# Edge scores of a graph network: ScalarE's copies for two tiles put ahead of others, VectorE's passes over fetched tiles placed in the units beside the last layer's chain

## The chip, the cores and the metric

The kernel runs on one core of a Trainium2 chip. The metric is the device time of one launch in microseconds (us). The median of three runs of the kernel before is 3469.57 us (3468.32 to 3470.26).

## The reference

64 graphs of 256 nodes with 256 features each go through four layers: first layer, second layer, attention, last layer (GNN[0], GNN[1], the attention layer, and LAST in the code). All graphs share one sparse 256x256 adjacency matrix. The first, second and last layer compute the same thing with weights of their own:

```python
pre_u = jnp.einsum('bud,dk->buk', h_t, W1[:d])
pre_v = jnp.einsum('bvd,dk->bvk', h_t, W1[d:])
hidden = jax.nn.relu(pre_u[:, :, None, :] + pre_v[:, None, :, :] + b1)
S = jax.nn.sigmoid(jnp.einsum('buvk,ko->buvo', hidden, W2)[..., 0] + b2[0])
a_t = jnp.einsum('buv,bud->bvd', S * A_a, h_t)
m_t = jnp.einsum('uv,bud->bvd', A_m, h_t) * h_t
z_t = beta1 * h_t + beta2 * (a_t @ Wa + ba) + beta3 * (m_t @ Wm + bm)
```

(The last line is shortened: the two products there are einsums.) The score S is wanted only where the adjacency matrix is not zero. The attention layer forms logits from one projected value per node, takes a softmax along the masked rows and adds the weighted features to its input.

## The kernel before, in words

**Edges.** At its start the kernel counts the edges and makes selection matrices from them. The edges off the diagonal are packed into tiles of up to 128 edges. For one edge the kernel needs pu of one node plus pv of the other, then a pass relu times W2 summed along the features. There are three ways to it. For the tiles in FAST, ScalarE copies rows of pu and pv into `pre` (rows_u, rows_v), and TensorE adds the pair of each edge with a selection matrix `pick` into a PSUM tile `ga`. For the tiles in FETCHED, POOL gathers rows from tables in HBM: tableu first, then tablev added on top of it (fetch, line 824). For the diagonal, `own` is pu + pv of the same node (itself). The few remaining edges share one gathered tile, `left`. Every tile holds two graphs, so it takes two VectorE passes (rated, both; in the profile `junk<-ga`, `junk<-fetched`, `junk<-own`, `junk<-left`), each of which writes one column of `raw`.

**From scores to sums.** rated_all turns a set of columns into `val` on ScalarE (tanh, then + 1) and on VectorE into `rm`. It is called twice in a unit: for EARLY, when the first half of the columns is there, and for LATE at the end. early() puts the remaining edges and the diagonal into `sa` (matmuls `ps<-ro,guo`). spread() brings `rm` into matrix form with 32 small matmuls in two halves (`ps<-rm,gu`) and adds it to `sa`. finish() forms sa x h, the output products and z.

**Streams and units.** Two streams, a and b, take two graphs each at a time, in 16 rounds. beside(heavy, light, placed) lays the scores of one stream's layer (heavy) beside the other stream's chain (light): the rest of its layer after the scores (after), attention, and the start of its next layer (before: pu, pv, tables in HBM, first copies into `pre`). Six such units make up a round. In the order of time the heavy parts are: a's first layer, b's first, a's second, b's second, a's last, b's last. The light chain is a generator; every step yields how many FAST tiles (made) and how many fetched tiles (got) are traced at that point. STEPS (line 45) holds these numbers for finish(), the list `beside` (line 656) those for before(). Beside b's last layer and a's first layer the light chain is the other stream's last layer and the start of its next graphs' first layer.

**What sets the order.** The order in which an engine issues its instructions is not the order of the code. A scheduler picks, per engine, among the instructions that its model holds to be ready, the one traced first. `issue_after(x)` adds an order behind x on x's engine, with no semaphore. With placed=True, `stay` puts TensorE's ga tiles, VectorE's passes and the EARLY tanh behind what was traced just before them on their engine, the diagonal is done beside the first two fetched tiles, and early() comes right after the EARLY ratings; otherwise the diagonal is done beside FAST tiles 1 and 2, the EARLY ratings come when all FAST tiles are traced, and early() follows the sixth fetched tile. In the kernel before, placed is True beside b's first layer and beside a's second.

**Names that matter.** FAST tile n uses pre[:, n]. before() calls rows_u(0, 2) and rows_v(4, 2) after its first half of nodes, and rows_v(0, 2) after its second. made() calls rows_u and rows_v for tiles 2n + 2 and 2n + 3, on ScalarE behind past[-1], the last rating of the unit before. `itself` does the diagonal. POOL's list of gathers (FETCHES) is one order across all units; the first six of a unit are issued in before(), behind the table writes of SP's queue (line 677), and the others at the start of the unit.

Of the kernel before, what the change touches and what calls it, by code (L numbers as in the profile page):

```python
# [17 lines left out]
GNN = ("L0_gnn_", "L1_gnn_", "L3_gnn_")  # L18
LAST = GNN[2]
# [25 lines left out]
STEPS = {  # L45
    GNN[0]: [(1, 1), (1, 1), (0, 1), (1, 0), (0, 1), (2, 1)],
    GNN[1]: [0, 0, 0, (0, 1), (0, 1), 1],
    LAST: [1, 1, (0, 1), (1, 1), (0, 1), (2, 1)],
}

VEC = {}
# [11 lines left out]
def blk(c):  # L63
    return slice(c * P, (c + 1) * P)
# [37 lines left out]
def adj_seq_kernel(ctx: ExitStack, tc: tile.TileContext, a: dict, out: bass.AP):  # L102
# [15 lines left out]
    tensor, vector, scalar = Noting(nc.tensor), Noting(nc.vector), Noting(nc.scalar)  # L118
# [383 lines left out]
    def few(stack):  # L502
# [139 lines left out]
        def more(st, l):  # L642

            return (st["side"], l) in (("a", LAST), ("b", GNN[1]))

        def before(st, l):

            hT = st["hT"]
            pu = one.tile([P, 2, 2, D], FP, tag="pu" + st["side"], name="pu")
            pv = one.tile([P, 2, 2, D], FP, tag="pv" + st["side"], name="pv")  # L650
            pre = one.tile([P, len(FAST), 2 * D], FP, tag="pre" + st["side"], name="pre")
            order = [(m, g) for m in range(2) for g in range(2)]
            if l == LAST:
                order = [(m, g) for g in range(2) for m in range(2)]

            beside = {LAST: [0, (0, 1), (0, 1), (0, 1)], GNN[1]: [0] + [(0, 1)] * 3, GNN[0]: [0, 0, (0, 2), (0, 1)]}[l]
            beside = dict(zip(order, beside))
            st["tables"] = [
                tables.tile([N, 2 * D], FP, tag="table" + t + st["side"], name="table" + t) for t in "uv"
            ]  # L660

            st["pu"], st["pv"], st["pre"] = pu, pv, pre
            if l != GNN[1]:
                st["own"] = one.tile([P, 2, 2, D], FP, tag="own", name="own")
            t = one.tile([P, FIRST, 2, D], FP, tag="fetched" + st["side"], name="fetched")
            st["fetched"] = [t[:, f] for f in range(FIRST)]
            for m, g in order:
                if l == LAST and (m, g) == (1, 0):
                    st["flip"](1)
                t = psum()  # L670
                for c in range(2):
                    mm(out=t, lhsT=hT[:, c, g, blk(m)], rhs=w1[l][:, c], start=c == 0, stop=c == 1)
                scalar.copy(pu[:, m, g, :], t[:, 0, :])
                vector.tensor_tensor(pv[:, m, g, :], t[:, 1, :], b1row[l], ALU.add)
                if g == 1:
                    for rows, x in zip(st["tables"], (pu, pv)):
                        nc.sync.dma_start(out=rows[blk(m)], in_=flat(x)[:, m])
                    if m == 0:
                        st["fetches"] = list(FETCHES_MORE if more(st, l) else FETCHES)

                        if numbered:
                            fetch(st, AHEAD)
                if l != GNN[1]:
                    vector.tensor_tensor(st["own"][:, m, g, :], t[:, 0, :], pv[:, m, g, :], ALU.add)
                if g == 1:
                    if m == 0:
                        rows_u(st, 0, 2, 0, 0)
                    rows_v(st, 4 - 4 * m, 2, 0)
                yield beside[(m, g)]
                if l == GNN[1] and (m, g) == (0, 1):  # L690
                    st["turn"](0)
                    yield 0, 1
                    st["turn"](1)
                    yield 0
            yield REST_OF_IT

            yield from mixed(st, l, later if past else None, (0,) if more(st, l) else (0, 1))

        def scores(st, l, placed):
# [3 lines left out]


            stay = behind if placed else lambda engine: nullcontext()
            pre = st["pre"]
            raw = wk.tile([P, LATE.stop], FP, tag="raw", name="raw")
            val = wk.tile([P, LATE.stop], FP, tag="val", name="val")
# [24 lines left out]
            def tile_scores(t, k, m, i):  # L733
                col = BLOCKS + 16 * m + 4 * k + i
                both(t, col, col + 8)
# [25 lines left out]
            def made():  # L761
                for n, (k, m, i) in enumerate(fast):
                    t = ga.tile([P, 2, D], FP, tag="ga", name="ga")
                    with stay(tensor):
                        mm(out=t, lhsT=pick[:, k, 4 * m + i, :], rhs=pre[:, n], start=True, stop=True)
                    tile_scores(t, k, m, i)
                    if 2 * n + 2 < len(fast):

                        with tc.issue_after(past[-1]) if past else nullcontext():
                            rows_u(st, 2 * n + 2, 2, *FAST[2 * n + 2][:2])  # L770
                            if n != 1:
                                rows_v(st, 2 * n + 2, 2, FAST[2 * n + 2][0])
                    if n in (1, 2) and not placed:
                        itself(n - 1)
                    count.append(n)
                    yield
                    if n == 2 and more(st, l):
                        yield from mixed(st, l, None, (1,), ga)

            def got(made):  # L780
                for f, block in enumerate(blocks):
                    if f == FIRST:
                        if placed:
                            while len(count) < 4:
                                next(made)
                        else:
                            for _ in made:
                                yield
                        with stay(vector):
                            rated(left, REST)  # L790
                        rated_all(EARLY, 0)
                        yield
                        if placed:
                            early(st)
                            yield
                    if f < 2 and placed:
                        itself(f)
                    with stay(vector):
                        tile_scores(fetched[f], *block)
                    if f == FIRST + 1 and not placed:  # L800
                        early(st)
                    yield
# [4 lines left out]

            made = made()
            return made, got(made), end

        def fetch(st, n):

            now, st["fetches"] = st["fetches"][:n], st["fetches"][n:]
            for f, x in now:
                rows = st["tables"][x]
                if f < 0:
                    to, ids = st["left"], (left_u, left_v)[x]
                    rows = rows.rearrange("n (g d) -> (n g) d", g=2)
                else:
                    to, ids = st["fetched"][f].rearrange("p g d -> p (g d)"), (ids_u, ids_v)[x][:, f : f + 1]  # L820
                    if f < FIRST:
                        rows = rows[blk(0)]
                with tc.issue_after(fetches[-1]) if fetches else nullcontext():
                    this = nc.gpsimd.indirect_dma_start(  # L824
                        out=to, out_offset=None, in_=rows, in_offset=bass.IndirectOffsetOnAxis(ap=ids, axis=0),
                        compute_op=(ALU.bypass, ALU.add)[x],
                    )
                fetches.append(this.ins)
# [9 lines left out]
        def rows_v(st, f, n, k):  # L838

            for n in range(f, f + n):  # L840
                i = FAST[n][2]
                scalar.copy(
                    st["pre"][halves[1 - k], n], st["pv"][halves[i % 2], i // 2].rearrange("p g d -> p (g d)")
                )
# [37 lines left out]
        def stream(side, starts):  # L882

            sts = [{"b": b, "side": side} for b in starts]
            load(sts[0])
            short = [before(sts[0], GNN[0])]
            for i, st in enumerate(sts):
                yield short, (st, GNN[0]), False
                yield [after(st, GNN[0]), before(st, GNN[1])], (st, GNN[1]), True
                yield [after(st, GNN[1]), attention(st), before(st, GNN[2])], (st, GNN[2]), False  # L890
                short = [after(st, GNN[2])]
                if i + 1 < len(sts):
                    load(sts[i + 1])
                    short = [halfway(after(st, GNN[2]), 4, before(sts[i + 1], GNN[0]), 2)]
            yield short, None, False
# [29 lines left out]
        past, numbered, fetches, later = [], [], [], []  # L925
# [119 lines left out]
```

## Time and profile before

| | |
|---|---|
| median of three runs | 3469.57 us |
| the profiled execution | 3468.32 us |
| its span | 3466.6 us |
| PE (matmuls) busy | 3361.7 us |
| VectorE (DVE) busy | 2639.6 us |
| POOL busy | 2416.1 us |
| weight loads (PEld) busy | 2067.6 us |
| ScalarE (ACT) busy | 1557.2 us |
| one copy pre<-pu for two tiles, mean | 1044 ns |
| one copy pre<-pv for one tile, mean | 616 ns |
| one pass over a fetched tile's graph, mean | 419 ns |
| one gather from tableu / tablev on POOL, mean | 1014 / 1583 ns |

The span is the time from the first to the last instruction. A row of the waits view reads "engine, what it was about to do, what it waited for: us in total, times, longest". A row of the timeline reads "start in us from the span's start, us, engine, operation, output<-inputs, count", and in brackets the engine's idle time before it with what ended it. Matmuls are pipelined, so that a matmul's bar is longer than the distance to the next one. An FP32 matmul in the code is two in the profile.

### The profile page before, as it was taken

To read this page: it belongs to the slowest core of one execution; us is meant where nothing else is said; L and a number is where in the kernel's file an instruction comes from. 1 tells how busy PE (TensorE), PEld (TensorE's weight loads), DVE (VectorE), ACT (ScalarE), POOL (GpSimd) and SP (SyncE) were. 2 spreads that over 40 slices of the span, in tenths; PEclk is the share of its full clock that TensorE was granted. 3 is DMA by queue.
4 is the path that set the end of the run, shared out by engine and by line. 5 is a ranking of instruction groups with operands and counts; after the bars stand their busy time and mean duration, and the time that the engine had idled before them with its cause. 6 is when DMAs were issued, how large, how long until landed. Compare 5 with 4: busy or idle time off the path is not lost.

```text
span 3466.6 us, 48384 instructions
## 1 busy us (share of the span) xinstructions
PE 3361.7 (97%) x14200; PEld 2067.6 (60%) x14200; DVE 2639.6 (76%) x10523; ACT 1557.2 (45%) x2833; POOL 2416.1 (70%) x1882
## 2 busy tenths in 40 slices
PE   6999999999999999999999999999999999999998
PEld 3566565565656566565665656656565665656655
DVE  5777787777777777777777877777777777777776
ACT  2444444444444444444444444444444444444442
POOL 3767777677767767677677776777767676776765
PEclk7999999999999999999999999999999999999999
DMA  5788787877878778787787877878787787877875
GB/s 148 164 185 188 166 207 164 193 176 178 197 168 196 179 178 186 176 196 171 178 188 165 197 170 187 183 170 205 167 196 173 178 197 165 193 179 175 190 162 129
DMA packets 289070, 620.81 MB, mean 179 GB/s; under 512 B 39072, under 2 KB 56352, under 8 KB 288800
## 3 DMA queue, kind: packets, MB, share of 16 engines
q0 software_dynamic: 204800, 461.49, 65.2%
q1 hardware_dynamic: 82416, 154.96, 12.8%
q8 instruction: 115, 1.88, 0.2%
q10 hardware_dynamic: 1584, 1.20, 0.1%
q14 instruction: 155, 1.27, 0.1%
HBM read 500.06 MB, written 117.44 MB: 178 GB/s over the span
## 4 chain that ended last, share of the span: by engine, by line
PE 68%; POOL 9%; DMA 7%; issue 7%; DVE 6%; ACT 3%; ACTq 0%; POOLq 0%; DVEq 0%
PE ps L79 52%; PE ga L79 16%; POOL fetched L824 8%; DMA fetched<-tablev,ids_v 4%; DVE junk L79 3%; ACT pre L79 2%; DMA fetched<-tableu,ids_u 2%; DVE rm L79 1%; DMA tableu<-pu 1%; POOL left L824 1%; DVE sa L79 1%; ACT val L79 1%; ACT pu L79 1%; DVE own L79 0%; DVE pv L79 0%
## 5 line engine op out<-in xcount | busy, mean ns | idle before, releaser
L824 POOL DMA_INDIRECT fetched<-tablev,ids_v x832 | 1317.3, 1583 | 381.1 <-issue 257.0
L824 POOL DMA_INDIRECT fetched<-tableu,ids_u x832 | 843.7, 1014 | 547.1 <-DMA tableu<-pu 286.7
L79 DVE SCALAR_TENSOR_TENSOR junk<-fetched,L_gnn_w2row 128x256 f32<-128x256 f32 x1664 | 643.0, 419 | 171.3 <-DMA fetched<-tablev,ids_v 167.3
L79 PE MATMUL ga<-pre,pick 128*128 128x512 f32 x1408 | 723.5, 609 | 37.0 <-ACT pre L79 27.4
L79 PE MATMUL ps<-L_gnn_w,hT 128*128 128x512 f32 x1536 | 708.0, 598 | 5.7 <-DMA hT<-in_xT_dram 5.7
L79 DVE SCALAR_TENSOR_TENSOR junk<-ga,L_gnn_w2row 128x256 f32<-128x256 f32 x1408 | 538.3, 419 | 103.7 <-PE ga L79 92.2
L79 PEld LDWEIGHTS ps<-L_gnn_w,hT 128*128 128x128 f32 x1536 | 280.6, 191 | 323.7 <-issue 300.2
L79 ACT COPY pre<-pv 64x512 f32<-64x512 f32 x704 | 434.0, 616 | 72.6 <-DVE pv L79 49.3
L79 PE MATMUL ps<-sa,h 128*128 128x256 f32 x1536 | 363.7, 382 | 13.2 <-DVE sa L79 8.9
L79 PEld LDWEIGHTS ps<-sa,h 128*128 128x128 f32 x1536 | 292.5, 191 | 126.0 <-issue 68.5
L79 ACT COPY pre<-pu 64x1024 f32<-64x1024 f32 x352 | 361.6, 1044 | 8.0 <-DVE ids_v L79 0.6
L79 PEld LDWEIGHTS ga<-pre,pick 128*128 128x128 f32 x1408 | 249.2, 191 | 184.4 <-issue 91.3
L79 ACT COPY pu<-ps 128x256 f32<-128x256 f32 x384 | 142.8, 372 | 481.3 <-PE ps L79 430.8
L79 ACT ACTIVATE hb<-hT,L_gnn_zbias,scas 128x512 f32<-128x512 f32 x128 | 97.3, 807 | 477.9 <-DVE hT L79 354.5
L79 DVE TENSOR_TENSOR rm<-gva,val 128x256 f32<-128x256 f32 x768 | 280.1, 420 | 33.1 <-ACT val L79 24.2
L79 PE MATMUL ps<-adj,h 128*128 128x256 f32 x1280 | 297.2, 384 | 4.0 <-issue 4.0
L79 PEld LDWEIGHTS ps<-adj,h 128*128 128x128 f32 x1280 | 242.1, 191 | 73.7 <-issue 40.3
L79 DVE TENSOR_TENSOR pv<-ps,L_gnn_b1row 128x256 f32<-128x256 f32 x384 | 161.7, 421 | 134.5 <-ACT pu L79 125.6
L79 PEld LDWEIGHTS ps<-rm,gu 128*64 128x64 f32 x3072 | 175.1, 138 | 135.2 <-issue 50.3
L79 ACT COPY aT<-ps 128x512 f32<-128x512 f32 x192 | 112.4, 585 | 315.9 <-PE ps L79 284.6
L79 PE MATMUL ps<-rm,gu 128*64 128x128 f32 x3072 | 218.7, 281 | 23.0 <-DVE rm L79 22.6
L79 PE MATMUL ps<-aT,L_gnn_Wa 128*128 128x512 f32 x512 | 240.6, 592 | 0.0
(149 smaller groups left out, 4211.8 us busy)
## 6 DMA issues: line engine op xcount, KB each, us to landing
tableu<-pu SPq DMA_DIRECT2D x192, 256.0 KB
tablev<-pv SPq DMA_DIRECT2D x192, 256.0 KB
hT<-in_xT_dram SPq DMA_DIRECT2D x32, 512.0 KB
h<-in_x_dram SPq DMA_DIRECT2D x64, 256.0 KB
out_dram<-h SPq DMA_DIRECT2D x64, 256.0 KB
fetched<-tableu,ids_u POOLq DMA_INDIRECT x832
fetched<-tablev,ids_v POOLq DMA_INDIRECT x832
L_gnn_w<-in_L_gnn_W_dram SPq DMA_DIRECT2D x6, 256.0 KB
```

The costliest lines, as they stand in the source:

```text
L79: self.last = getattr(self.engine, op)(*a, **k)
L824: this = nc.gpsimd.indirect_dma_start(out=to, out_offset=None, in_=rows, in_offset=bass.IndirectOffsetOnAxis(ap=ids, axis=0), compute_op=( ...
```

## The change

Three edits stand in the diff. First, before() notes its last copy into `pre` as st["rows"], and made() puts the copies for tiles 2 and later behind it on ScalarE. Second, placed becomes True beside a's first layer from the second round on (`i > 0`). The same value is used beside b's last layer of every round but the last through the stream's next step: both units have the other stream's last-layer chain as their light part. What the diagonal does is split off: only b's first layer and a's second (diagonal_later) keep it beside the fetched tiles. Third, the step lists of the last layer's finish() and of the first layer's before() change where fetched tiles are traced.

```diff
-    LAST: [1, 1, (0, 1), (1, 1), (0, 1), (2, 1)],
+    LAST: [1, (1, 1), 0, (1, 1), (0, 1), (2, 1)],
...
-            beside = {LAST: [0, (0, 1), (0, 1), (0, 1)], GNN[1]: [0] + [(0, 1)] * 3, GNN[0]: [0, 0, (0, 2), (0, 1)]}[l]
+            beside = {LAST: [0, (0, 1), (0, 1), (0, 1)], GNN[1]: [0] + [(0, 1)] * 3, GNN[0]: [(0, 1)] * 4}[l]
...
                         rows_u(st, 0, 2, 0, 0)
                     rows_v(st, 4 - 4 * m, 2, 0)
+                    st["rows"] = scalar.last.ins
...
+            diagonal_later = placed and (st["side"], l) in (("b", GNN[0]), ("a", GNN[1]))
...
-                        with tc.issue_after(past[-1]) if past else nullcontext():
+                        with tc.issue_after(past[-1]) if past else nullcontext(), tc.issue_after(st["rows"]):
                             rows_u(st, 2 * n + 2, 2, *FAST[2 * n + 2][:2])
...
-                    if n in (1, 2) and not placed:
+                    if n in (1, 2) and not diagonal_later:
                         itself(n - 1)
...
-                    if f < 2 and placed:
+                    if f < 2 and diagonal_later:
                         itself(f)
...
-                yield short, (st, GNN[0]), False
+                yield short, (st, GNN[0]), i > 0
```

## The prediction

> **What bounds the kernel now.** I call a unit by its heavy stream and layer (a-first, b-first, a-second, b-second, a-last, b-last, the order in time; 16 rounds). A unit ends where ScalarE rates its last score columns (the 128x16 tanh into val); fifteen rounds between such marks give 211.4 us each.
>
> First the page's busy times, then the view of waits for TensorE's matmul row (total us, times, longest):
>
> ```profile
> PE 3361.7 (97%) x14200; PEld 2067.6 (60%) x14200; DVE 2639.6 (76%) x10523; ACT 1557.2 (45%) x2833; POOL 2416.1 (70%) x1882
> ```
>
> ```profile
> PE ga L79 <- ACT pre L79: 27.4, 25, 2.3
> PE ps L79 <- DVE rm L79: 22.6, 27, 6.0
> ```
>
> TensorE is the bound and its visible waits are small: what can be won is in these two rows. A busy row hides part of a wait, so I took starts of successive matmuls from the timeline and subtracted the usual spacing (429 ns after 128x512, 216 after 128x256, 54 after one of the rm,gu pairs). What is over 350 ns per gap sits at unit starts: a-last 16 gaps, 1.23 to 2.55 us, 27.4 us in all; b-last 16 gaps, 8.3 us (0.47 to 0.90); b-first 16 gaps, 13.8 us (mostly 0.65). The rest is scattered, or in the first 100 and last 30 us.
>
> Then the timeline at the start of one a-last unit, ScalarE and then TensorE (start, us, instruction, count, idle time before):
>
> ```profile
> 1463.20 0.22 ACT L79 ACTIVATE val<-val 128x16 f32<-128x16 f32 x1
> 1463.44 1.04 ACT L79 COPY pre<-pu 64x1024 f32<-64x1024 f32 x1
> 1464.51 2.53 ACT L79 COPY pre<-pv 64x512 f32<-64x512 f32 x4
> ```
>
> ```profile
> 1465.18 1.12 PE L79 MATMUL ga<-pre,pick 128*128 128x512 f32 x2 [1.04 <-ACT pre L79]
> 1466.23 1.09 PE L79 MATMUL ps<-rm,gu 128*64 128x128 f32 x16
> 1467.26 1.13 PE L79 MATMUL ga<-pre,pick 128*128 128x512 f32 x2
> ```
>
> The first edge tile (ga) starts when the first pre<-pv copy ends (1465.13). In front of that copy stands pre<-pu, the 1.04 us copy for tiles 2 and 3, which nobody needs yet. The order is the same at all 16 starts of a-last and b-last; at the other four kinds of start both pv copies are already done before the tanh.
>
> Last, TensorE at the start of one b-first, and of the a-first of the same round:
>
> ```profile
> 1570.43 1.09 PE L79 MATMUL ps<-rm,gu 128*64 128x128 f32 x16
> 1571.96 1.42 PE L79 MATMUL ps<-rm,gu 128*64 128x128 f32 x16 [0.43 <-issue]
> ```
>
> ```profile
> 1539.37 1.13 PE L79 MATMUL ga<-pre,pick 128*128 128x512 f32 x2
> 1540.93 1.42 PE L79 MATMUL ps<-rm,gu 128*64 128x128 f32 x16 [0.44 <-DVE rm L79]
> ```
>
> The second half of the spread waits for rm, which follows val, which follows VectorE's last passes over fetched tiles. a-first (free order) fills with a ga tile; b-first (placed) can't.
>
> **What the skill says.** The Trainium skill, "TensorE: Matmul & The Clock Gate", Architectural detail, calls ScalarE's and VectorE's queues strict FIFO: the trace agrees (pv stood 1.04 us behind pu though ready). "Perfetto Trace Analysis", Identifying the Most-Contended Engine, says that matmul busy time is no good measure of headroom and weight-load time is; here 60% against 97%, but most of the distance is spacing that no reordering removes. "DMA: Bandwidth & Descriptors", Anatomy of one DMA — SWDGE path, gives 2.0 us + bytes/436 GB/s, an estimate of 2.6 us for 256 KB. From the trace's DMA records (each gather ends with sixteen 4-byte packets) a v gather here takes 4.7 us from issue to the last of them (4.2 to 6.0), a u gather 3.8: the measured ones are used. The same page, Two DMAs through the same engine are not ordered, asks for a wait between dependent transfers: POOL's 127.8 us of waits on u gathers agree.
>
> **The change, part by part.** Waits other than those named stay as they are.
> 1. ScalarE's edge (copies for tiles 2 on behind the copies for tiles 0 and 1). It adds no instruction. At a-last the order becomes v0, v1, u2, v2, v3. v0 ends at 1463.44 + 0.62 = 1464.06, so the first ga runs from 1464.11, not 1465.18. The spread's second half follows at 1465.16, but rm's third pass ends at about 1465.2: 1465.26 against 1466.23. Next ga tile: v1 done at 1464.70, no wait. Gain 0.95 a start, x16 = 15.2 us. In starts with a 2.5 us gap VectorE was late with pv behind a fetch; the 1.04 us comes off all the same. At b-last, v0 would end at 1505.27 and TensorE is busy until 1505.91: the whole 0.47 to 0.50 goes, x16 = 7.5 to 8. u2 and v2 are needed at 1508.5 and end by 1507.6. What is queued behind the edge is u2 alone, whose tiles come later.
> 2. Placed order in b-last and in a-first from round two. At the start of a-first the ga tile no longer fills the gap: it is pinned behind the spread. From b-first, placed today, I read: with rm in time, sums of A times h (sa,h) start 2.80 us after the spread's first half; with rm late, 1.74 + 3.17 = 4.91 us after val. Today's free a-first needs some 4.4 us for the same work undelayed, so fewer switches win about 0.4 to 0.7.
>    VectorE's tail after the last pv of a-first holds half a tile's passes, own, four sa (1.65), two tiles (1.4): 4.0 us to val. Placed: own and three tiles, 0.34 + 3 x 0.69 = 2.4, since the early ratings and sa move to mid-unit, into idle times of 2.17 and 1.27 us. So val comes up to 1.3 us sooner, but not before the last gather's landing + 1.2 us (the least seen). Now val follows that landing by 1.2 to 4.2 us at b-last (under 1.8 in 7 of 15 rounds) and 1.3 to 4.7 at a-first.
>    Taking the later of the two for each round, with TensorE 0.5 us earlier from part 1: a-first's start loses 4.7 us over 15 rounds (in the example landing 1537.4, val 1538.6, sa,h 1543.5 against 1543.25), b-first's start gains 11.9 (sa,h 1574.2 against 1575.13), a-second's loses 0.7.
> 3. The step lists (last layer: f0 beside the second aT, and so on; first layer: one fetched tile per step) only place VectorE passes and cost no instruction. The mid-unit tiles land ahead of their slot by 0.6 us or more (b-last in one round: f1 to f3 landed 12.9, 15.6, 18.3 us after the start; their slots, behind the two pv and the first output's matmuls, are at about 14.5, 16.3, 19). If a landing is later, pv or the output sum waits; TensorE has three ga and five ps buffers in front.
>    Round one's a-first stays free; its end follows the last landing by 1.8 us: 0, at worst +-2.
>    No DMA is added or moved past another: POOL's list is the same, and gathers start from table writes that come earlier with TensorE.
>
> Sum: 15.2 + 7.5 (fifteen b-lasts; the sixteenth is swallowed by the tail's landings) - 4.7 + 11.9 - 0.7 = 29 us. With VectorE's advance only 0.6 us, the same working gives 21. I take 25: the profiled execution goes from 3468.3 (span 3466.6, 1.7 around it) to 3443.3; the median of the runs stands 1.3 above it, so 3444.5.
>
> **The rivals.**
> - Only ScalarE's edge pays, 0.27: the gathers of b-last, a-first and b-first run back to back on POOL from one table write, so val cannot come sooner, and pinned ga tiles lose what b-first wins. For: seven b-last rounds have val at 1.2 to 1.8 after landing. Against: b-first's gap of 0.65 is there also where the lag is 3 us. Time 3450 to 3463, about 3455.
> - Strict placing turns landings into VectorE stalls, slower, 0.12: a gather that lands after its slot blocks pv and the table write behind it, so the next unit's gathers start later, and the delay returns. Today's placed units show the wait (junk on fetched, 167.3 us, 129 times) without TensorE stopping. It decides above 23/30 = 0.77 us of TensorE idle in each of the 30 newly placed units (23 being part 1's gain); at 1.5 us it is 30 x 1.5 - 23 = +22, 3491.
> - The edge does nothing, because the issue order that comes out has pu first or another stall in the place (rm at a-last is only 0.1 us behind), and placing nets zero: 0.06, 3463 to 3476.
>
> **How the numbers follow.** Likeliest case 0.55 (3430 to 3450; own range); the others 0.27, 0.12, 0.06. A measurement tells from no change about 0.2%, 6.9 us. Faster: 0.55 + 0.27 = 0.82; same 0.06; slower 0.12. The range 3430 to 3466 leaves out the slower case, half of the unchanged one and a small tail below.
>
> **What would show it.** Right: pre<-pv twice directly after val at a-last and b-last; PE ga on ACT pre from 27.4 to under 10 us; a-last's starts 0.9 shorter; the rm wait at b-first gone; four sa and the early val some 5 us earlier in b-last and a-first. Wrong: a new rm gap of about 1 us at a-first's start; junk-on-fetched waits growing by over 60 us with pv behind them; b-first's gap unchanged.

## The result and the profile after

The changed kernel takes 3462.8 us (median; 3458.0 to 3467.5) beside 3468.3 us for the kernel before on the same chip: ratio 0.9985, 95% interval 0.9976 to 0.9994. That is 5.5 us less, within the 0.2% that a measurement tells from no change, where 25 us less were predicted. Measured again in the first set below, the ratio is 0.9980 (0.9969 to 0.9991), so a small gain is real.

The profiled execution took 3460.8 us (span 3459.1). Its busy times:

```profile
PE 3354.6 (97%) x14200; PEld 2069.3 (60%) x14200; DVE 2649.2 (77%) x10523; ACT 1555.9 (45%) x2833; POOL 2414.1 (70%) x1882
```

The largest waits of TensorE's matmul row, and VectorE's wait for fetched tiles (total us, times, longest):

```profile
PE ps L79 <- DVE rm L79: 18.6, 10, 5.8
PE ps L79 <- DVE sa L79: 18.2, 16, 2.3
PE ga L79 <- ACT pre L79: 16.0, 16, 1.7
...
DVE junk L79 <- DMA fetched<-tablev,ids_v: 179.5, 134, 3.8
```

The wait of ga on pre fell from 27.4 to 16.0 us, not to under 10. The wait on rm hardly fell (22.6 before), and the one on sa doubled (8.9 before).

The timeline at the start of one a-last, ScalarE and then TensorE; it is the same round as the one shown of the kernel before:

```profile
1465.72 0.22 ACT L79 ACTIVATE val<-val 128x16 f32<-128x16 f32 x1
1465.96 1.26 ACT L79 COPY pre<-pv 64x512 f32<-64x512 f32 x2
1467.12 1.04 ACT L79 COPY pre<-pu 64x1024 f32<-64x1024 f32 x1
...
1465.59 0.65 PE L79 MATMUL ps<-rm,gu 128*64 128x128 f32 x6
1466.63 1.13 PE L79 MATMUL ga<-pre,pick 128*128 128x512 f32 x2 [0.39 <-ACT pre L79]
1467.69 1.74 PE L79 MATMUL ps<-rm,gu 128*64 128x128 f32 x26
```

ScalarE's order is the one predicted: two pv copies directly behind val. TensorE's order is not. Before, the ga tile stood behind 16 matmuls of the spread; now it stands behind 6, with 26 after it. The scheduler picks the tile earlier (I take it that its model now holds the tile ready earlier; this was not looked at), so less work covers the wait that is left.

TensorE at the starts of one a-first and one b-first:

```profile
1325.03 1.02 PE L79 MATMUL ga<-pre,pick 128*128 128x512 f32 x2
1325.98 1.09 PE L79 MATMUL ps<-rm,gu 128*64 128x128 f32 x16
1328.98 1.22 PE L79 MATMUL ps<-rm,gu 128*64 128x128 f32 x15 [1.90 <-DVE rm L79]
...
1572.81 2.35 PE L79 MATMUL ps<-rm,gu 128*64 128x128 f32 x32
```

b-first's spread now runs through without a wait (32 in a row). At a-first the wait for rm stands in the middle of the spread, up to 3.0 us, and no ga tile fills it.

To see where time moves I sum, over the last 15 rounds, what the distance between two matmul starts has over its usual value, wherever that is more than 300 ns (us):

| where | before | after |
|---|---|---|
| a-last's start, ga behind the spread | 26.2 | 18.3 |
| b-last's start, ga behind adj,h | 7.8 | 0.0 |
| b-first's start, spread for rm | 13.4 | 0.0 |
| a-first's start, spread for rm | 2.7 | 16.2 |
| all gaps | 75.3 | 68.6 |

The first three rows give 29.1 us. A-first's start takes 13.5 back, and sums with an sa that VectorE finishes late some 12 more (the last section has these). How the loss is split differs between executions: in a second profile of the changed kernel (after_again, below) no sa comes late, and a-first's wait is 32.7 us.

### The profile page after: what moved, and what is told of

It is laid out like the page before. It is cut to its first block, busy times and chain, and to the rows that moved or that the text cites. A ratio compares the mean times of both kernels' runs of the same rounds, so it can differ in the third digit from the quotient of the medians.

```text
span 3459.1 us, 48323 instructions
## 1 busy us (share of the span) xinstructions
PE 3354.6 (97%) x14200; PEld 2069.3 (60%) x14200; DVE 2649.2 (77%) x10523; ACT 1555.9 (45%) x2833; POOL 2414.1 (70%) x1882
## 4 chain that ended last, share of the span: by engine, by line
PE 80%; POOL 6%; DMA 5%; issue 4%; DVE 3%; ACT 2%; another core or an unknown queue 0%; ACTq 0%; POOLq 0%; SPq 0%; DVEq 0%
PE ps L79 62%; PE ga L79 17%; POOL fetched L827 5%; DMA fetched<-tablev,ids_v 3%; DVE junk L79 1%; DMA tableu<-pu 1%; ACT pre L79 1%; DVE sa L79 1%; POOL left L827 1%; DMA fetched<-tableu,ids_u 1%; ACT val L79 0%; ACT pu L79 0%; DVE rm L79 0%; ACT logits L79 0%; DVE scratch L79 0%
## 5 line engine op out<-in xcount | busy, mean ns | idle before, releaser
L79 DVE SCALAR_TENSOR_TENSOR junk<-fetched,L_gnn_w2row 128x256 f32<-128x256 f32 x1664 | 639.0, 419 | 184.0 <-DMA fetched<-tablev,ids_v 179.5
L79 PEld LDWEIGHTS ps<-sa,h 128*128 128x128 f32 x1536 | 292.7, 192 | 141.9 <-issue 68.6
L79 PEld LDWEIGHTS ps<-adj,h 128*128 128x128 f32 x1280 | 243.4, 190 | 75.1 <-issue 40.9
L79 PE MATMUL ps<-mT,L_gnn_Wm 128*128 128x512 f32 x512 | 240.6, 592 | 0.0
```

Of the source, the lines that this page charges most:

```text
L79: self.last = getattr(self.engine, op)(*a, **k)
```

## The experiments

Four sets were run, each on one chip beside runs of the kernel before. That kernel's own median was 3470.2, 3454.6, 3452.3 and 3461.9 us in them, so times are compared within a set, and ratios are to the kernel before of the set. A ratio is the recorded one; the quotient of the two medians differs from it by up to 0.0008, some 3 us.

### First set: the parts alone

`edge_only` keeps of the change only ScalarE's edge (st["rows"] and the second issue_after). `placed_only` keeps all but the edge:

```diff
-                        with tc.issue_after(past[-1]) if past else nullcontext(), tc.issue_after(st["rows"]):
+                        with tc.issue_after(past[-1]) if past else nullcontext():
```

`after_again` is the changed kernel. `half_first` is the changed kernel with the first ga tile beside a-last traced behind the spread's first half, which brings back TensorE's order of 16 spread matmuls, ga, 16 spread matmuls (in after() and spread()):

```diff
-            yield 1
+            yield 0 if (st["side"], l) == ("b", GNN[1]) else 1
...
                 it = vector.tensor_tensor(sa[:, m], sa[:, m], t, ALU.add)
+                if m == 0 and (st["side"], l) == ("b", GNN[1]):
+                    yield 1
```

> The kernel before with ScalarE's edge alone. Theory A (the edge gains 8 us at the starts of a-last, 8 us at those of b-last, and keeps all of it; the placing as a whole gives some of it back): time 3450 to 3455 us, 14 to 18 below before; PE ga on ACT pre some 16 to 20 us; the gap between adj,h and ga at b-last under 1 us in sum. Theory B (what the edge gains at the start of a unit is lost later in the same unit to sums of sa that VectorE adds late, whatever is placed): 3461 to 3466 us, with the waits of ps<-sa,h on sa grown to about 18 us as in the changed kernel.

> The changed kernel without ScalarE's edge. Theory A (placing gains 12 us at the starts of b-first, loses 10 at those of a-first and 10 or more to late sums in mid-unit): 3472 to 3480 us, 4 to 12 above before. Theory B (placing is worth what its starts show, +10 - 12, and the edge nothing): 3463 to 3468 us. My prediction's own figure for this part was about -6 (4.7 - 11.9 + 0.7 us).

> The changed kernel itself, beside the others on the same chip. Time 3458 to 3466. If the late sums of sa (TensorE waiting 0.7 to 2.3 us at ps<-sa,h) come from the program's order, they return in the same rounds of b-last and a-second as in the first profile; if they come from the chip's moment (memory, instruction supply), they move to other rounds.

> The changed kernel, with the first ga tile beside a-last traced behind the spread's first half instead of before the spread, so that TensorE's order is rm,gu x16, ga, rm,gu x16 again (in the profile's count), as my prediction assumed. Theory A (the reordering halved the edge's gain at a-last): the gap before ga at a-last falls from 0.61 to about 0.1 us, 16 x 0.5 = 8 us less: 3453 to 3457 against 3461 to 3463. Theory B (VectorE's rm, then sa, sets the first sa,h of a-last, so that the tile's place is of no account): sa,h starts 4.7 us after adj,h as now and the time is that of the changed kernel within 2 us.

| kernel | median us | ratio (95%) |
|---|---|---|
| edge_only | 3469.7 | 0.9998 (0.9988 to 1.0008) |
| placed_only | 3461.6 | 0.9980 (0.9971 to 0.9989) |
| after_again | 3466.0 | 0.9980 (0.9969 to 0.9991) |
| half_first | 3463.3 | 0.9978 (0.9968 to 0.9987) |

Theory A in these texts is that the edge keeps what it gains at the starts; theory B, that late sums of sa take it. Theory A falls at once: the edge, for which I had 22.7 us, is worth nothing that can be told from noise, and the placing is worth all that the change is (7 us by the ratios; my own sum for it was 6.5). Theory B is nearer with its 3461 to 3466 us for edge_only, but too low, and its cause is not there: in this set no sum of sa comes late by more than 0.5 us, in any of the four profiles, the changed kernel's included.

The gap sums say where the edge's gain went. The last column is a second run of the edge alone, from the fourth set; the second column is a second profile of the kernel before:

| start of | before | before_again | edge_only | edge_only_2 |
|---|---|---|---|---|
| a-last, ga | 26.2 | 24.3 | 14.9 | 16.1 |
| b-last, ga | 7.8 | 9.3 | 1.2 | 0.0 |
| a-first, rm | 2.7 | 1.3 | 21.6 | 18.6 |
| b-first, rm | 13.4 | 10.0 | 15.0 | 18.0 |
| b-second, rm | 4.8 | 1.3 | 8.2 | 7.7 |

The gain is there, some 17.5 us at the two starts. It comes back as waits for rm in the units behind, most of it at a-first. The waits view of edge_only shows it as a whole, where the kernel before had 22.6 and 167.3 us:

```profile
PE ps L79 <- DVE rm L79: 46.8, 45, 5.6
...
DVE junk L79 <- DMA fetched<-tablev,ids_v: 247.1, 191, 4.2
```

In half_first the gap at a-last falls from 17.1 (after_again) to 9.2, as theory A expected, and its ratio stays. Where these 7.9 us go is not shown: b-last's gap grows by 3.5 us and a-first's wait for rm does not grow (32.7 and 30.5), and the two profiled executions are far apart (3453.5 us, the fastest of 22, against 3471.3), so that their gap sums can't be set against each other.

What rm waits for at a-first, in one round of edge_only_2, TensorE and then VectorE:

```profile
1331.51 1.12 PE L79 MATMUL ga<-pre,pick 128*128 128x512 f32 x2
1334.56 1.42 PE L79 MATMUL ps<-rm,gu 128*64 128x128 f32 x16 [1.93 <-DVE rm L79]
...
1331.97 0.43 DVE L79 SCALAR_TENSOR_TENSOR junk<-fetched,L_gnn_w2row 128x256 f32<-128x256 f32 x1 [1.34 <-DMA fetched<-tablev,ids_v]
1332.32 0.08 DVE L79 DVE_READ_ACCUMULATOR junk<-fetched,L_gnn_w2row 128x1 f32 x1
1332.32 0.42 DVE L79 SCALAR_TENSOR_TENSOR junk<-fetched,L_gnn_w2row 128x256 f32<-128x256 f32 x1
...
1333.41 1.43 DVE L79 TENSOR_TENSOR rm<-gva,val 128x256 f32<-128x256 f32 x4
```

VectorE is free and waits 1.34 us for the last fetched tile of b-last. Two passes, tanh and rm follow, and TensorE waits for them. So in this round the last landing of b-last's gathers sets the start of a-first, and an earlier start of b-last moves it only if its gathers start earlier too. Over all 15 rounds val (the start of its tanh) follows a-last's last landing by 1.33 us on average with the edge (2.02 in the kernel before), and b-last's by 1.54 (2.24); the second profile of the kernel before has 1.63 and 2.26. About 1.2 us is the least seen anywhere, so of the 0.8 and 1.0 us of slack that the kernel before had there (0.4 and 1.1 in the second profile), 0.1 and 0.3 are left.

Why the stream of gathers doesn't start earlier either is seen at the boundary of a-last and b-last in edge_only: POOL's rows, and between them the write of the table by SP's queue.

```profile
1506.64 1.54 POOL L825 DMA_INDIRECT fetched<-tablev,ids_v  x1 [1.66 <-DMA fetched<-tableu,ids_u]
...
1509.57 0.33 SPq L677 DMA_DIRECT2D tableu<-pu  x1
...
1512.70 0.98 POOL L825 DMA_INDIRECT fetched<-tableu,ids_u  x1 [4.52 <-DMA tableu<-pu]
```

The first row is a-last's last gather. The write of b-last's table is issued 2.9 us after that gather, and POOL waits for it until 3.1 us after its issue. The DMA records have this write's landing in 25 rounds of edge_only, after_again and edge_only_2 together. In 19 of them it follows the landing of a-last's last gather by 0.96 to 1.15 us, in the other six by 1.3 to 2.4 us; in none does it come sooner.

That is no rule for every table write. Those of a-first and b-first, issued while POOL goes on with the other unit's gathers, land 2.8 to 5.9 us after their issue (68 records of the same three runs), and at least 9 us before the last of these gathers does. In the 25 rounds b-last's is issued only 0.2 to 3.3 us before the last landing. There, a write that is issued earlier lets the first gather start hardly sooner: in half_first ScalarE's pu copy in front of it comes 0.5 us earlier in the unit than in after_again (37.15 against 37.69 us after a-last's start), and the first gather comes 0.43 us later behind it (3.95 against 3.52 us).

The Trainium skill, "DMA: Bandwidth & Descriptors", Queues, rings and completion order, says that a transfer's completion signal lands only behind every earlier write of the same DMA engine, across its queues. The nearly constant distance of b-last's write agrees with that, and so do the writes of a-first and b-first, which land about as long after their issue as a gather does (4.0 us on average; the prediction has 3.8 and 4.7 for the gathers). No run here isolates it, and the one record that half_first has shows 0.5 us.

### Second set: shorter streams

Theory G: the streams of gathers close right behind TensorE's work in a-last and b-last and take what the edge gains. Theory V: VectorE's own order takes it. The last two gathers from tablev are left out in both units. Their tiles then hold pu alone, so their scores are other numbers; every pass stays.

```diff
-                        st["fetches"] = list(FETCHES_MORE if more(st, l) else FETCHES)
+                        st["fetches"] = list(FETCHES_MORE if more(st, l) else FETCHES)[: -2 if l == LAST else None]
```

> The kernel before itself, profiled on the same chip as the three others. Ratio 1 within 0.1%. Both theories: its val at the ends of a-last and b-last follows the last gather's landing by about 2 us on average (2.02 and 2.24 in the first profile), its wait for rm at a-first's start is small (2.7 us in 15 rounds), its gap before ga at a-last 26 us.

> The kernel before with the last two gathers from tablev left out in the units a-last and b-last (those of tiles 8 and 9, and of 6 and 7): these tiles get pu alone, so that their scores are other numbers; every pass over them stays. The stream of gathers of these two units ends some 3 us sooner. Theory G (the stream of gathers, table write to last landing, closes just behind VectorE in these units): before has 0.8 to 1 us of slack there, so little comes of it: 3450 to 3467 us. Theory V (VectorE's and TensorE's own order sets the ends of these units): the same within 5 us of before.

> ScalarE's edge alone, with the same four gathers left out (the same tiles get pu alone). Theory G (what the edge gains at the starts of a-last and b-last waits at their ends for the last gather): with the stream shorter the gain comes through, 14 to 22 us below the kernel before with the same gathers left out; the wait for rm at a-first's start falls from 21.6 us to under 8; the first table write of b-last lands 2.0 to 2.5 us after its issue instead of 3.1. Theory V (VectorE's order takes the gain back): the edge is worth 0 to 5 us here as well, and the wait for rm at a-first stays near 20 us.

> The changed kernel with the same four gathers left out (the same tiles get pu alone). Theory G: the whole of the change is worth 16 to 29 us against the kernel before with the same gathers left out, since my 25 us supposed that the gathers do not hold the units up. Theory V: it is worth the 5 to 7 us that it is worth with all gathers.

| kernel | median us | ratio (95%) |
|---|---|---|
| before_again | 3458.4 | 1.0004 (0.9991 to 1.0016) |
| before_short | 3447.1 | 0.9976 (0.9967 to 0.9985) |
| edge_short | 3429.9 | 0.9928 (0.9910 to 0.9946) |
| after_short | 3423.2 | 0.9911 (0.9894 to 0.9928) |

Beside shorter streams the edge is worth 17.2 us (3447.1 - 3429.9) and the whole change 23.9, close to the predicted 25 (the sum that stood behind it was 29). The shorter streams alone give 7.5 us (11.3 beside before_again), a little more than theory G had: the kernel before was held up by its gathers in part as well. The wait for rm at a-first is 1.1 us in edge_short, and its waits view has:

```profile
PE ps L79 <- DVE rm L79: 9.6, 12, 4.2
...
DVE junk L79 <- DMA fetched<-tablev,ids_v: 162.4, 103, 3.4
```

The first gather of b-last starts 2.37 us after the issue of its table write, where it is 3.46 in edge_only (landings themselves are not recorded in this trace). Theory V falls.

### Third set: all gathers, in another order

Theory G points to an edit that leaves nothing out. POOL waits in front of the v gather of tile 0 until tile 0's u gather has landed (0.6 us a round in a-last, some 2 in a-first and b-first), and in a-last in front of tile 9's v gather (0.9 us; the 1.66 in the rows above is one of them). Another u gather can stand in these places:

```diff
-FETCHES = [(0, 0), (1, 0), (2, 0), (0, 1), (3, 0), (1, 1)]
+FETCHES = [(0, 0), (1, 0), (2, 0), (3, 0), (0, 1), (1, 1)]
...
-FETCHES_MORE = FETCHES[:-2] + [(8, 0), (6, 1), (9, 0), (7, 1), (8, 1), (9, 1)]
+FETCHES_MORE = FETCHES[:-2] + [(8, 0), (9, 0), (6, 1), (7, 1), (8, 1), (9, 1)]
```

> The kernel before with its gathers in another order, all of them there: the u gather of tile 3 ahead of the v gather of tile 0 (POOL waits there 0.6 us in a-last, 0.4 in b-last, some 2 in a-first and b-first), and the u gather of tile 9 ahead of the v gather of tile 6 (POOL waits 0.9 us at tile 9's v gather in a-last). Theory G: the streams of a-last and b-last end about 1.5 and 0.4 us sooner, but before has slack there; with the shorter streams of a-first and b-first 3 to 10 us below before. Theory P (the order in which tiles land matters more to VectorE's passes than the end of the stream): same as before or slower.

> ScalarE's edge alone, with the gathers in that other order. Theory G: the edge is now worth something without leaving anything out: 8 to 17 us below before_order, since a-last's stream gives up 1.5 us and b-last's 0.4; a-first's wait for rm falls from 21.6 us to 5 to 12. Theory P: edge_order within 4 us of before_order, the wait at a-first as it was.

> The changed kernel with the gathers in that other order. Theory G: edge and placing add up again, 17 to 30 us below before and 10 to 22 below the changed kernel. Theory P: as the changed kernel within 5 us.

> As after_order, and in addition the first ga tile beside a-last behind the spread's first half (half_first's edit). Theory G: at a-last another 0.5 us a round is saved at the start, and counts only where the stream of gathers ends early enough: 0 to 8 us below after_order. If a-last is still held by its gathers: equal to after_order within 2 us.

| kernel | median us | ratio (95%) |
|---|---|---|
| before_order | 3441.2 | 0.9968 (0.9955 to 0.9981) |
| edge_order | 3429.9 | 0.9927 (0.9911 to 0.9943) |
| after_order | 3424.8 | 0.9928 (0.9913 to 0.9942) |
| half_order | 3423.6 | 0.9916 (0.9902 to 0.9929) |

The new order alone is worth 11.1 us (before_order), just above the 3 to 10 that theory G had. The edge is worth 11.3 us on top of it by the medians (14 by the ratios), and the wait for rm at a-first with the edge is 6.3 us instead of 21.6. Theory P falls. POOL's waits for u gathers, in edge_only_2 and then in edge_order:

```profile
POOL fetched L825 <- DMA fetched<-tableu,ids_u: 142.3, 133, 3.8
...
POOL fetched L825 <- DMA fetched<-tableu,ids_u: 50.7, 77, 2.6
```

edge_order, after_order and half_order leave nothing out and beat both kernels of this case (0.9927, 0.9928 and 0.9916 against 0.9980 for the change). Their intervals don't tell them apart, so the placing and half_first's edit add nothing certain on top of the edge and the new order, where theory G had edge and placing adding up again. In half_order a-last's gap falls, from 14.9 to 7.2, and a-first's rises from 13.9 to 21.2.

The chain of work that ended last points the same way. Its shares for before, edge_only and edge_order:

```profile
PE 68%; POOL 9%; DMA 7%; issue 7%; DVE 6%; ACT 3%; ACTq 0%; POOLq 0%; DVEq 0%
```

```profile
PE 51%; POOL 17%; DMA 12%; issue 10%; DVE 7%; ACT 2%; POOLq 0%; ACTq 0%; DVEq 0%; SPq 0%
```

```profile
PE 79%; DVE 5%; POOL 4%; DMA 4%; issue 3%; ACT 2%; POOLq 0%; DVEq 0%; ACTq 0%
```

With the edge alone POOL and DMA carry 29% of the chain instead of 16%; with the other order of gathers, 8%. But the share differs between executions of one kernel: it is 22% in edge_only_2, and 11% and 26% in the two profiles of the changed kernel. It is a hint, not a measure.

### Fourth set: which stream

The edge alone and the shorter streams had run on different chips. This set puts them on one, and shortens one unit's stream at a time: `edge_short_a` leaves out a-last's two v gathers, `edge_short_b` b-last's.

```diff
-                        st["fetches"] = list(FETCHES_MORE if more(st, l) else FETCHES)[: -2 if l == LAST else None]
+                        st["fetches"] = list(FETCHES_MORE if more(st, l) else FETCHES)[: -2 if (st["side"], l) == ("b", LAST) else None]
```

> ScalarE's edge alone, once more, beside the three others on one chip. Theory G (the last gathers of a-last and b-last take the edge's gain): 0 to 6 us below before, with 10 us or more of waits for rm at a-first's start. Other cases of theory G fall if it is worth 12 us or more here.

> ScalarE's edge with the last two v gathers of a-last and of b-last left out (these tiles get pu alone), once more. Theory G: 20 to 27 us below before, and 15 or more below the edge alone on the same chip.

> ScalarE's edge with the last two v gathers left out in a-last only (tiles 8 and 9 get pu alone). If a-last's stream alone holds the pair of units up (b-last's stream starts behind it and has room once it starts sooner): nearly all of edge_short_2's gain, within 5 us of it. If b-last's own stream holds as well: about half.

> ScalarE's edge with the last two v gathers left out in b-last only (tiles 6 and 7 get pu alone). If a-last's stream alone counts: within 4 us of the edge alone. If it is the sum of the two streams, from a-last's first gather to b-last's last landing, that counts: nearly all of edge_short_2's gain here as well, as in edge_short_a.

| kernel | median us | ratio (95%) |
|---|---|---|
| edge_only_2 | 3459.9 | 0.9994 (0.9985 to 1.0003) |
| edge_short_2 | 3427.1 | 0.9897 (0.9880 to 0.9913) |
| edge_short_a | 3450.4 | 0.9962 (0.9948 to 0.9976) |
| edge_short_b | 3427.9 | 0.9901 (0.9887 to 0.9916) |

On one chip the edge is worth 2 us beside the full streams, and with the edge the kernel is 32.7 us faster beside the shorter ones. (It is then 34.7 us below the kernel before, where theory G had 20 to 27.) b-last's stream alone gives all of that, a-last's about a third. None of the three patterns that I had put down fits: neither a-last's stream alone, nor half and half, nor the sum of the two.

The same round's a-first in edge_short_b, TensorE and then VectorE:

```profile
1319.40 1.09 PE L79 MATMUL ps<-rm,gu 128*64 128x128 f32 x16
1320.42 1.13 PE L79 MATMUL ga<-pre,pick 128*128 128x512 f32 x2
1321.48 0.32 PE L79 MATMUL ps<-rm,gu 128*64 128x128 f32 x1
...
1319.18 0.43 DVE L79 SCALAR_TENSOR_TENSOR junk<-fetched,L_gnn_w2row 128x256 f32<-128x256 f32 x1
1319.53 0.09 DVE L79 DVE_READ_ACCUMULATOR junk<-fetched,L_gnn_w2row 128x1 f32 x1
1319.53 0.49 DVE L79 SCALAR_TENSOR_TENSOR hb<-h,scas,zbrow 128x256 f32<-128x256 f32 x1
```

VectorE's last pass over a fetched tile waits for nothing, and the spread's second half follows the ga tile at once. b-last in numbers (us, means of 15 rounds):

| | first gather to last landing | last landing to val | unit |
|---|---|---|---|
| before_again | 32.62 | 2.26 | 34.96 |
| edge_only_2 | 33.04 | 1.55 | 34.78 |
| edge_order | 32.26 | 2.06 | 34.17 |
| edge_short_b | 28.66 | 4.97 | 33.72 |

b-last's stream counts most because POOL goes from it into a-first's and b-first's streams without a pause (0.30 us between them in edge_only_2, against pauses of 2.7 to 6.2 us before the streams of a-second, b-second, a-last and b-last itself): three streams hang on one first gather. In edge_short_b the waits for rm are 3.5 us at a-first, 10.2 at b-first and 0.8 at b-second, against 18.6, 18.0 and 7.7 in edge_only_2: 29.8 of the 32 us. Part of this would come without the edge as well: shorter streams alone gave 7.5 us in the second set. Whether b-last's stream gives that part too was not run.

## Why the prediction was wrong, point by point

- **What bounds the kernel.** "TensorE is the bound and its visible waits are small: what can be won is in these two rows." The two rows were read rightly, but a wait that is won at one place is time only if nothing else sets the end of that stretch. Val sets the end of a unit, and in a-last and b-last it had 0.8 and 1.0 us over the least distance from the last landing (0.4 and 1.1 in the second profile).
- **The step that failed: part 1, "Gain 0.95 a start, x16 = 15.2" and "x16 = 7.5 to 8".** 22.7 us were counted at the starts; 0 to 2 were measured (edge_only, edge_only_2). The gain at the starts is some 17 us, and the wait for the last gather takes it back. Part 2 of the same prediction holds val at "the last gather's landing + 1.2 us". What kept part 1 out of that limit is one sentence: "gathers start from table writes that come earlier with TensorE". The writes do come earlier and the gathers don't. After a-last's start, b-last's first table write is issued at 38.8 us in the kernel before and at 38.1 with the edge (38.6 and 38.2 in the second profiles), and its first gather starts at 41.5 in both (41.6 and 41.4). Beside shorter streams both move by 0.6 us (39.1 to 38.5, 41.5 to 40.9), and the step gives 17.2 us.
- **Its size also was too large.** a-last's gap sum fell by 10.2 us in 15 rounds between before_short and edge_short, not by 14.3 (15 x 0.95), since TensorE's ga tile moved forward in the spread. half_first and half_order put it back, which halves the gap (17.1 to 9.2, 14.9 to 7.2).
- **"Waits other than those named stay as they are."** VectorE's wait for fetched tiles was 167.3 us before and 247.1 and 228.7 in the two runs of the edge alone.
- **Part 2, the placing, -6.5 by its sum (4.7 lost at a-first, 11.9 won at b-first, 0.7 lost at a-second).** Right: -8.6 by the medians of placed_only (-6.9 by the ratio), -6.7 from edge_short to after_short. In that pair a-first's wait for rm grew by 4.8 us and b-first's fell by 10.1. Beside the full streams a-first's wait grew by more than the 4.7 (to 15.7 us in placed_only), but the prediction counted in starts of sa,h, and there it holds: from each unit's first sa,h to the next one's, placed_only has +4.5 us at a-first, -10.6 at b-first and +0.4 at a-second in 15 rounds against the first profile of before (+5.2, -7.2 and +0.4 against the second, which is of another chip). Val does come sooner, as predicted: at the end of b-last it follows the last landing by 1.36 instead of 2.24 us, and the unit takes 34.38 instead of 34.97 us.
- **Part 3, the step lists, 0.** Consistent with the above, not measured alone.
- **The rivals.** "Only ScalarE's edge pays" had the right mechanism, "the gathers of b-last, a-first and b-first run back to back on POOL from one table write, so val cannot come sooner", and charged it to the wrong part: it is the edge that pays nothing. Its "seven b-last rounds have val at 1.2 to 1.8 after landing" (the records give eight) was the evidence. "Strict placing" did not come about in the time, though the growth of waits that it named did in one of two profiles: junk on fetched, 167.3 us before, was 179.5 with the change and 246.3 in after_again. With the edge alone it was 247.1 and 228.7 and with the placing alone 210.7, so it isn't the placing that makes it. "The edge does nothing" was right about the edge's worth, for a reason that it didn't name, and wrong about the placing.
- **What would show it.** Right: pv twice after val, the rm gap at b-first gone, and the four sa and the early val sooner in b-last (both by 5.1 us) and a-first (4.5 and 4.4). Wrong: ga on pre at 16.0 us, a-last's starts 0.5 us shorter instead of 0.9, and the gap of about 1 us at a-first, which I had named as the sign of failure.

## What to carry to other kernels

Before a gain at the start of a stretch is added to a sum, ask what ends the stretch, and put every part of the change under the same limit: here the last landing of the gathers plus 1.2 us. Where the chains of two engines end within a microsecond of each other in a unit, as here, the kernel has two bounds, and an edit on one may pay only together with an edit on the other: the edge gave 0 to 2 us alone and 11 to 17 beside gathers that end sooner, while the other order of gathers gave 11 us even alone. The shares in the chain of work that ended last (POOL and DMA 16% beside TensorE's 97% of busy time) hinted at the second bound; the distance from the last landing to val, held against its least value, shows it. Then look for waits inside the second chain: here two changed places in the list of gathers let the edge pay 11 us.

## What was not expected of the hardware

B-last's table write, issued on SP's queue up to 3.3 us before the last of a-last's gathers lands, lands about 1.0 us after it (19 of 25 recorded rounds), and issuing it 0.5 us earlier moved the gather behind it by 0.1 us. Table writes that are issued while gathers go on for long land 2.8 to 5.9 us after their issue (68 records).

In the first pair of profiles VectorE's second sum into sa started late with nothing visible before it, and TensorE waited for it (issue and remote stand where the profile names nothing that ended the wait):

```profile
1397.12 0.70 PE L79 MATMUL ps<-sa,h 128*128 128x256 f32 x2 [0.23 <-DVE sa L79]
1400.09 1.56 PE L79 MATMUL ps<-sa,h 128*128 128x256 f32 x6 [2.28 <-issue]
...
1399.35 0.69 DVE L79 TENSOR_TENSOR sa<-sa,ps 128x512 f32<-128x512 f32 x1 [2.29 <-remote]
```

Such gaps over 0.5 us sum to 13.7 us in 15 rounds of the kernel before and 25.5 of the changed one. In the second set's four profiles they sum to 4.9 to 9.7 us. In the other twelve, the changed kernel's second one among them, there is none. It isn't the program's order, then; what it is stays open. Time per round did not show it: the change measures the same with it (0.9985) and without (0.9980).
